# Cross-attention for 16 batches on one core: A of the last heads by 11 block products, and the steps without A in the order of the others

## The chip, the cores and the metric

The kernel runs on one core of a Trainium2 chip. The time is the device time of one execution in microseconds, taken as the median of several runs. The engines are named as the profile names them: PE is TensorE (matmuls; PEld is its weight load), DVE is VectorE, ACT is ScalarE, POOL is GpSimd and SP is SyncE, which issues most DMAs. Each engine works through its own queue in order and waits for the others by semaphores.

## The reference

All is float32, with B = 16 batches, 256 queries of width 256, 77 keys of width 192, and 8 heads of width 256:

```
Q = x @ Wq;  K = c @ Wk;  V = c @ Wv            # split into 8 heads
score = Q K^T / sqrt(256), masked;  attn = softmax(score)
ctx = attn V;  out = ctx @ Wo + x
return layernorm(out) * gamma + beta
```

The kernel never forms Q, K or V. For each head it makes G = Wk Wq^T / 16 once (tiles gA, gB, gC, and sums of their blocks in gS) and U = Wv Wo once (uA, uB). For each batch it makes A = G c (the 256 x 77 matrix whose product with x gives the scores) and VW = c U. A tile is 128 queries of one batch, so a batch is two tiles, and tile t belongs to batch t // 2.

## The kernel before, in words

For one batch the work is this, with the functions' names.

- A for its batch and all heads, made on TensorE for groups of four batches (g = 0 to 3) and pairs of heads. There are two ways. `prepare_fast(g, u)` makes A of a pair of heads for all four batches by a block scheme with 11 products in place of 12 for each head; VectorE puts the blocks together in four additions a head (`put_together`), and ScalarE copies one block a head. `prepare_a` makes it directly, and ScalarE copies the result. The bank is called pf in the first way and pa in the second.
- VW: `prepare_vw(b)`, two parts on TensorE (part_A over 128 rows, part_B over the other 64), then two copies on ScalarE into vw.
- `scores(t)`: TensorE, x against A, into banks ps. `shift(t)`: VectorE subtracts from the bias and takes the minimum. `exponential(t)`: ScalarE, eight activations. `weigh(t)`: VectorE's reciprocal of the sums (rden), then POOL multiplies in two pieces (four for the two tiles of a batch). `turn(t)`: VectorE transposes the result into pT.
- `seven(b)`: the product of the weighted scores of both tiles with VW on TensorE by a scheme of seven block products (banks pm and po). It needs sums of pT blocks (`sums(b)`, four additions on POOL, tile ss) and differences of VW blocks (`differences(b)`, one subtraction on POOL, tile ts). Its first product uses pT and vw alone, its second ss and vw, its third and fourth ss and ts. ScalarE copies pm to m. Then `add_products(b)` on VectorE and `add_blocks(b)` on POOL (five additions) add all to x.
- The last two batches and a last one in halves use `attend` instead, a plain product.
- `finish(t)`: mean and variance, on ScalarE by two activations where `by_act(t)` holds, else on VectorE (bn_stats, bn_aggr). `spread` and `invert` make the reciprocal of the deviation, `normalise(t)` the output row, and SP stores it. `statistics` is finish, spread and invert of a batch.

The schedule is written by hand: instructions are put on each engine's queue in the order in which the text emits them, and the tile framework adds the semaphores. [...]

Up to batch 8 steps come in pairs. `long_step(b)` (odd b) does the scores of batch b + 1, VW of batches b + 1 and b + 2, seven(b), and two calls of prepare_fast for later batches; `short_step(b + 1)` does the scores of batch b + 2 and seven(b + 1). POOL's work in a long step, in the order of the text, is sums(b) (left over from the short step before), weigh of the two tiles of batch b + 1, add_blocks(b - 1), sums(b + 1), add_blocks(b), differences(b + 1), differences(b + 2), and at times the sums of c for the next group (`sums_of_c`); weigh of batch b + 2 follows in the short step. Lists `behind` and `between` hold work that is emitted in the next step.

From batch 9 on (`ready = 9`) a plain loop emits one step for each batch. Steps 9 to 12 make what is missing of A for the last group (heads 4 to 7) with `prepare_a`, in pieces of one pair of heads and two batches, together with VW of two batches in every other step (`ahead`); there differences(b + 1) comes ahead of seven(b) and of the additions. Steps 13 and 14 end with attend.

Of the kernel before, what the change touches and what calls it, by code (L numbers as in the profile page):

```python
# [20 lines left out]
GB = 4  # L21
# [6 lines left out]
def kernel(  # L28
# [14 lines left out]
    B, S, DI = x.shape  # L43
# [3 lines left out]
    NG = B // GB  # L47
    QT = S // P
# [55 lines left out]
    NS = B - GB // 2 - 1  # L104

# [278 lines left out]
    def prepare_vw(b, rest_first=False):  # L384

        vw_of[b] = vwp.tile([P, 4, 2, P], F32, tag="vw", name=f"vw_{b}", bufs=3)
        parts = slice(0, 4) if b < NS else slice(1, 5)
        pv = [ps_mm.tile([P, 2 * DI], F32, tag="mm", name=f"pv_{b}_{k}") for k in range(2)]

        def part_A():  # L390
            for k in range(2):
                for i in range(NM):
                    nc.tensor.matmul(  # L393
                        pv[k][i * BK : (i + 1) * BK],
                        cA[:, b, k * BK : (k + 1) * BK],
                        uA[:, parts, :, i],
                        start=not rest_first,
                        stop=rest_first,
                    )

        def part_B():
            for i in range(NM):
                for k in range(2):
                    nc.tensor.matmul(  # L404
                        pv[k][i * BK : (i + 1) * BK],
                        cB[half(k), b, k * BK : (k + 1) * BK],
                        uB[half(k), parts, :, i],
                        start=rest_first,
                        stop=not rest_first,
                    )  # L410

        def copies():
            return [
                (vw_of[b][:, :, k, :], pv[k].rearrange("p (q d) -> p q d", q=4)) for k in range(2)
            ]

        return part_A, part_B, copies
# [80 lines left out]
    def by_act(t):  # L498
        return t // QT < B - 2 * GB - 1

    def fast(b):
        return b < B - GB - GB // 2
# [146 lines left out]

    def add_seven(b):  # L650

        add_products(b)
        add_blocks(b)
# [485 lines left out]
    def work_of(b, rest_first=False):  # L1139
        g, n = b // GB + 1, b % GB  # L1140
        work = [prepare_vw(b, rest_first)]
        if b <= NS and not fast(b):
            part = (0, 2) if g < NG else (2, GB)
            work.append(prepare_a(NG - 1, (NF // 2 + n % 2,), *part, rest_first))
        return work

# [12 lines left out]

    def turn_x_and_normalise(g, n, old):  # L1160
        turn_some_x(g, n)
        if old:
            normalise(old[1])
# [25 lines left out]
    def long_step(b):  # L1189
# [12 lines left out]
        works = work_of(b + 1) + work_of(b + 2)  # L1202
# [6 lines left out]
        fasts = []  # L1209
        for k in range(2):  # L1210
            fasts.append(prepare_fast(g, n + k))
            if k == 0:
                copy_out(works[:1])
            fasts[k][0]()
            if k == 0:
                copy_out(works[1:])
# [9 lines left out]
        else:  # L1226
# [10 lines left out]
            for k in range(2):  # L1237
                differences(b + 1 + k)
# [8 lines left out]
        fasts[0][1](0)  # L1247
        fasts[0][1](1)
        fasts[1][1](0)
        behind.append(partial(fasts[1][1], 1))  # L1250
# [3 lines left out]
    def short_step(b):  # L1254
# [15 lines left out]
        def last_turn():  # L1270
            turn(new[1])
            sums(b + 1)
# [6 lines left out]
    ready = B - GB - GB // 2 - 1  # L1279
# [5 lines left out]
    for b in range(ready, B - 1):  # L1285
        old = range(max(b - 1, 0) * QT, b * QT)
        now = range(max(b, 0) * QT, (b + 1) * QT)
        new = range((b + 1) * QT, (b + 2) * QT)
# [3 lines left out]
        g, n = (b + 1) // GB + 1, (b + 1) % GB  # L1292
        if g < NG and n % 2 == 0:
            load_x((g * GB + n) // 2)
        alone = b + 1 >= B - GB // 2
        ahead = not alone and n % 2 == 0
        works = work_of(b + 1) if alone or ahead else []
        for part_A, *_ in works:
            part_A()
        for _, part_B, _ in works:  # L1300
            part_B()
# [22 lines left out]
        if ahead:  # L1324
            copy_out(works)
        spread(old[0], old[-1] + 1)
        if ahead:
            works = work_of(b + 2, rest_first=True)
            for _, part_B, _ in works:
                part_B()  # L1330
            for part_A, *_ in works:
                part_A()
        copy_out(works)
        if b + 1 < NS:
            differences(b + 1)
        if ahead and g < NG:
            load_xT(g * GT + n * QT, g * GT + (n + 1) * QT, after_pool=True)
        if b < NS:
            seven(b)
            invert(old[0], old[-1] + 1)  # L1340
            normalise(old[0])
            for t in new:
                turn(t)
            if alone or ahead:
                turn_x_and_normalise(g, n, old)
                if ahead and g < NG:
                    load_xT(g * GT + (n + 1) * QT, g * GT + (n + 2) * QT)
            else:
                behind.append(partial(turn_x_and_normalise, g, n, old))
            if ahead:  # L1350
                sums(b + 1)
            add_seven(b)
            if b + 1 < NS and not ahead:
                sums(b + 1)
            continue
# [53 lines left out]
```

## Time and profile before

| | us |
|---|---|
| median of 3 runs (268.94 to 269.13) | 268.95 |
| the profiled execution | 268.58 |
| its span, first to last instruction | 266.8 |
| TensorE busy in it | 260.5 |
| VectorE busy | 212.7 |
| GpSimd busy | 191.5 |
| ScalarE busy | 166.9 |

The profile is of one execution; its span lies 1.8 us inside its time. A timeline row has its start and its length in us from the start of the span, the engine, the line of the kernel, the operation, the tile written and the tiles read, and a count; consecutive instructions of one kind are one row. A float32 matmul has two records. The chain of waits follows the work that ended last back to the start; its rows in order of time give a start, a length and what ran.

### The profile page before, as it was taken

Reading aid. Unit: us, or ns where it says so; the run is one execution under the profiler, and the core shown is the slowest. Engines: PE = TensorE matmul, PEld = TensorE weight load, DVE = VectorE, ACT = ScalarE, POOL = GpSimd, SP = SyncE. Lnnn points to the kernel's source line nnn. Section 1 sums busy time; section 2 is a strip of 40 time slices with the busy share of each in tenths; the row PEclk is TensorE's granted clock in tenths of the full one; section 3 lists DMA queues with packets and bytes.
Section 4 is the critical chain, followed back from the end, with each engine's and each line's share of the span. In section 5 each row is a group of like instructions: output and inputs, shape, how many; then the busy total and the mean of one; then the engine's idle time right before and its main releaser. Section 6 shows DMA issues by size and latency. Waiting matters only on the chain.

```text
span 266.8 us, 15067 instructions
## 1 busy us (share of the span) xinstructions
PE 260.5 (98%) x6330; PEld 202.8 (76%) x6330; DVE 212.7 (80%) x860; ACT 166.9 (63%) x710; POOL 191.5 (72%) x272
## 2 busy tenths in 40 slices
PE   7999999999999999999999999999999999999992
PEld 6566578948986899679967996799669957985662
DVE  0554968479893789988997969898988798799785
ACT  3253548624584689648983798467964595636772
POOL 1042098799459896899479996997699899685452
PEclk9999999999999999999999999999999999999999
DMA  6999997900240002131314012221234010100112
GB/s 188 209 206 225 335 148 160 300 18 4 63 104 5 2 6 66 58 90 37 83 43 122 5 24 65 81 85 41 54 127 132 20 44 2 44 23 25 42 43 80
DMA packets 41699, 22.73 MB, mean 85 GB/s; under 512 B 24144, under 2 KB 40608, under 8 KB 41632
## 3 DMA queue, kind: packets, MB, share of 16 engines
q1 hardware_dynamic: 41248, 20.98, 31.3%
q0 software_dynamic: 384, 0.79, 1.3%
q8 instruction: 50, 0.82, 1.3%
q14 instruction: 17, 0.14, 0.2%
HBM read 17.57 MB, written 4.19 MB: 82 GB/s over the span
## 4 chain that ended last, share of the span: by engine, by line
PE 96%; DMA 2%; DVE 1%; SPq 0%; issue 0%; DVEq 0%
PE ps L469 25%; PE pf L361 11%; PE po L622 11%; PE pv L393 10%; PE pm L622 9%; PE pv L404 6%; PE pa L203 5%; PE po L555 4%; PE pu L956 3%; PE pa L215 2%; PE pr L429 2%; PE pgb L1017 2%; DMA wq_nat<-in_L_xattn_Wq_dram 2%; PE pw L970 1%; PE pr L440 1%; PE phb L1033 1%
## 5 line engine op out<-in xcount | busy, mean ns | idle before, releaser
L512 ACT ACTIVATE s<-s,top 128x77 f32<-128x77 f32 x256 | 85.2, 346 | 24.5 <-DVE top L486 24.5
L469 PE MATMUL ps<-a,xT 128*32 128x154 f32 x2048 | 70.1, 294 | 0.0
L469 PEld LDWEIGHTS ps<-a,xT 128*32 128x32 f32 x2048 | 65.8, 110 | 2.0 <-issue 1.5
L533 POOL TENSOR_TENSOR p<-s,rden 128x512 f32<-128x512 f32 x64 | 47.7, 769 | 21.9 <-DVE rden L527 21.7
L486 DVE CUSTOM_DVE_ANT_0 s<-ps,bias 128x77 f32<-128x77 f32 x256 | 43.3, 232 | 4.6 <-PE ps L469 4.0
L512 ACT ACTIVATION_READ_ACCUMULATOR s<-s,top 128x1 f32 x224 | 41.9, 187 | 0.0
L373 DVE TENSOR_TENSOR a<-pf,a 128x154 f32<-128x154 f32 x80 | 33.9, 435 | 7.3 <-PE pf L361 4.9
L664 POOL TENSOR_TENSOR xg<-xg,m 128x256 f32<-128x256 f32 x39 | 28.8, 738 | 2.7 <-DVE xg L676 0.7
L543 DVE STREAM_TRANSPOSE pT<-p 128x640 f32<-128x640 f32 x32 | 26.3, 827 | 5.1 <-POOL p L533 5.0
L393 PE MATMUL pv<-uA,cA 128*32 128x512 f32 x256 | 29.6, 593 | 0.0
L1150 ACT COPY vw<-pv 128x512 f32<-128x512 f32 x32 | 17.1, 587 | 14.9 <-PE pv L404 14.9
L760 DVE SCALAR_TENSOR_TENSOR xg<-xg,rstd,bet 128x256 f32<-128x256 f32 x27 | 22.7, 840 | 2.6 <-ACT rstd L711 1.2
L586 POOL TENSOR_TENSOR ts<-vw 128x768 f32<-128x768 f32 x13 | 23.6, 1831 | 0.0
L486 DVE DVE_READ_ACCUMULATOR2_ANT top<- 128x1 f32 x256 | 20.9, 82 | 0.0
L393 PEld LDWEIGHTS pv<-uA,cA 128*32 128x32 f32 x256 | 8.0, 110 | 13.3 <-issue 9.8
L731 DVE SCALAR_TENSOR_TENSOR xg<-xg,mv,gam 128x256 f32<-128x256 f32 x30 | 18.0, 600 | 0.1
L361 PE MATMUL pf<-cT,gS 64*64 64x154 f32 x240 | 17.4, 290 | 0.0
L603 POOL TENSOR_TENSOR ss<-pT 128x256 f32<-128x256 f32 x13 | 9.7, 745 | 9.8 <-DVE pT L543 9.7
L404 PE MATMUL pv<-uB,cB 64*32 64x512 f32 x256 | 16.3, 596 | 0.0
L622 PE MATMUL po<-vr,pT 128*32 128x256 f32 x208 | 16.0, 379 | 0.0
L361 PEld LDWEIGHTS pf<-cT,gS 64*64 64x64 f32 x240 | 15.8, 133 | 0.0
L203 PE MATMUL pa<-cA,gA 128*32 128x308 f32 (+1 forms) x256 | 14.0, 360 | 0.0
(153 smaller groups left out, 543.1 us busy)
## 6 DMA issues: line engine op xcount, KB each, us to landing
xg<-in_x_dram SPq DMA_DIRECT2D x8, 512.0 KB, 4.4
xT<-in_x_dram SPq DMA_DIRECT2D x56, 64.0 KB, 2.7
out_dram<-xg SPq DMA_DIRECT2D x11, 256.0 KB, 2.7
wo<-in_L_xattn_Wo_dram SPq DMA_DIRECT2D x4, 512.0 KB, 7.9
wq_blk<-in_L_xattn_Wq_dram SPq DMA_DIRECT2D x12, 128.0 KB, 4.6
out_dram<-xg SPq DMA_DIRECT2D x10, 128.0 KB, 1.7
wk_blk<-in_L_xattn_Wk_dram SPq DMA_DIRECT2D x12, 96.0 KB, 4.0
wvT<-in_L_xattn_Wv_dram POOLq DMA_DIRECT2D x8, 96.0 KB, 6.3
```

The lines of the kernel that those rows point to most:

```text
L203: nc.tensor.matmul(flat(o[i * BK : (i + 1) * BK]), gA[:, h, cols(dc, i)], flat(cA[:, batches, :]), start=not rest_first and n in opening, ...
L361: nc.tensor.matmul(bank[half(i), n], weight(i), moving, start=start, stop=stop,)
L373: nc.vector.tensor_tensor(out, *of, ALU.add)
L393: nc.tensor.matmul(pv[k][i * BK : (i + 1) * BK], cA[:, b, k * BK : (k + 1) * BK], uA[:, parts, :, i], start=not rest_first, stop=rest_first,)
L404: nc.tensor.matmul(pv[k][i * BK : (i + 1) * BK], cB[half(k), b, k * BK : (k + 1) * BK], uB[half(k), parts, :, i], start=rest_first, stop=n ...
L469: nc.tensor.matmul(ps[m // 2][i * BK : (i + 1) * BK, m % 2 * 2 * S2 : (m % 2 + 1) * 2 * S2], xT_of[t // PT][:, j * NM + m, dc], flat(a_of[ ...
L486: nc.vector.tensor_tensor_reduce(s[:, h], ps[a][:, k * S2 : (k + 1) * S2], bias[:, b, :], scale=-1.0, scalar=FAR, op0=ALU.add, op1=ALU.min ...
L512: nc.scalar.activation(s[:, h], s[:, h], AF.Exp, bias=top[:, one], scale=-1.0, accum_out=den[:, one] if summed_by_act(t) else None,)
L533: nc.gpsimd.tensor_tensor(part, e_mh[:, :, :, keys], rden_mh.unsqueeze(3).to_broadcast(list(part.shape)), ALU.mult,)
L543: nc.vector.transpose(pT_of[t].rearrange("p n m q -> p m n q"), p.rearrange("p m (n k) -> p m n k", k=BK),)
L622: nc.tensor.matmul(out[i * BK : (i + 1) * BK], weight[:, i], moving, start=first and n == 0, stop=final and n == len(terms) - 1,)
L664: nc.gpsimd.tensor_tensor(to, to, what, ALU.add)
```

## The change

The pairs of long and short steps go on to batch 12 (`ready = NS = 13`). Three things follow. The last group's heads 4 to 7 are made by prepare_fast, in long step 9, and the four calls of prepare_a in steps 9 to 12 go. Long step 11, which has no A left to make, emits all else in the order of the other long steps; what belongs to batch 13 in `differences` and `sums` is left out there, since that batch uses attend. And `by_act`, which is tied to `ready`, now holds up to batch 10 in place of batch 6. The branches of the plain loop that served steps 9 to 12 go, with their helpers; steps 13 and 14 stay. The diff, cut to its core:

```diff
+    ready = NS
...
     def by_act(t):
-        return t // QT < B - 2 * GB - 1
-
-    def fast(b):
-        return b < B - GB - GB // 2
+        return t // QT < ready - 2
...
-    def work_of(b, rest_first=False):
-        g, n = b // GB + 1, b % GB
-        work = [prepare_vw(b, rest_first)]
-        if b <= NS and not fast(b):
-            part = (0, 2) if g < NG else (2, GB)
-            work.append(prepare_a(NG - 1, (NF // 2 + n % 2,), *part, rest_first))
-        return work
...
     def long_step(b):
...
-        works = work_of(b + 1) + work_of(b + 2)
+        works = [prepare_vw(b + 1 + k) for k in range(2)]
         for part_A, *_ in works:
             part_A()
         if now:
             seven(b)
         for _, part_B, _ in works:
             part_B()
-        fasts = []
-        for k in range(2):
-            fasts.append(prepare_fast(g, n + k))
-            if k == 0:
-                copy_out(works[:1])
-            fasts[k][0]()
-            if k == 0:
-                copy_out(works[1:])
+        fasts = [prepare_fast(g, n)] if g < NG else []
+        copy_out(works[:1])
+        for products, _ in fasts:
+            products()
+        copy_out(works[1:])
+        if fasts:
+            fasts.append(prepare_fast(g, n + 1))
+            fasts[1][0]()
...
             add_blocks(b - 1)
             turn(new[0])
             add_products(b)
             turn(new[1])
             sums(b + 1)
             add_blocks(b)
             for k in range(2):
-                differences(b + 1 + k)
+                if b + 1 + k < NS:
+                    differences(b + 1 + k)
...
-        fasts[0][1](0)
-        fasts[0][1](1)
-        fasts[1][1](0)
-        behind.append(partial(fasts[1][1], 1))
+        if fasts:
+            fasts[0][1](0)
+            fasts[0][1](1)
+            fasts[1][1](0)
+            behind.append(partial(fasts[1][1], 1))
...
     def short_step(b):
...
             turn(new[1])
-            sums(b + 1)
+            if b + 1 < NS:
+                sums(b + 1)
             add_products(b)
             if b + 1 == ready:
                 add_blocks(b)
...
-    ready = B - GB - GB // 2 - 1
     for b in range(-1, ready, 2):
         long_step(b)
         short_step(b + 1)
...
     for b in range(ready, B - 1):
...
-        alone = b + 1 >= B - GB // 2
-        ahead = not alone and n % 2 == 0
-        works = work_of(b + 1) if alone or ahead else []
+        works = [prepare_vw(b + 1)]
...
-        if b + 1 < NS:
-            differences(b + 1)
-        if ahead and g < NG:
-            load_xT(g * GT + n * QT, g * GT + (n + 1) * QT, after_pool=True)
-        if b < NS:
-            seven(b)
-            invert(old[0], old[-1] + 1)
-            normalise(old[0])
-            for t in new:
-                turn(t)
...
-            if ahead:
-                sums(b + 1)
-            add_seven(b)
-            if b + 1 < NS and not ahead:
-                sums(b + 1)
-            continue
         for t in now:
             attend(t)
```

More of the change, by code (lines that the diff above doesn't have):

```diff
@@ L382, in prepare_fast, with prepare_vw @@
         return products, put_together
-    def prepare_vw(b, rest_first=False):
+    def prepare_vw(b):
         vw_of[b] = vwp.tile([P, 4, 2, P], F32, tag="vw", name=f"vw_{b}", bufs=3)
@@ L396, in part_A @@
                         uA[:, parts, :, i],
-                        start=not rest_first,
-                        stop=rest_first,
+                        start=True,
+                        stop=False,
                     )
@@ L407, in part_B @@
                         uB[half(k), parts, :, i],
-                        start=rest_first,
-                        stop=not rest_first,
+                        start=False,
+                        stop=True,
                     )
@@ L648, in seven @@
         m_of[b] = m
-    def add_seven(b):
-        add_products(b)
-        add_blocks(b)
     def add_products(b):
@@ L1158, in turn_some_x @@
                 transpose_x(to_turn[0] * GT + j)
[L1160 to L1163, printed above, removed]
     assert QT == 2
@@ L1285 @@
     for b in range(ready, B - 1):
-        old = range(max(b - 1, 0) * QT, b * QT)
-        now = range(max(b, 0) * QT, (b + 1) * QT)
-        new = range((b + 1) * QT, (b + 2) * QT)
+        old, now, new = (tiles_of(b + i) for i in (-1, 0, 1))
         scores_and_masks(new, old if b == B - 2 else ())
@@ L1291 @@
             behind.pop(0)()
-        g, n = (b + 1) // GB + 1, (b + 1) % GB
-        if g < NG and n % 2 == 0:
-            load_x((g * GB + n) // 2)
-        alone = b + 1 >= B - GB // 2
-        ahead = not alone and n % 2 == 0
-        works = work_of(b + 1) if alone or ahead else []
-        for part_A, *_ in works:
+        works = [prepare_vw(b + 1)]
+        for part_A, part_B, _ in works:
             part_A()
-        for _, part_B, _ in works:
             part_B()
@@ L1323 @@
             weigh(t)
-        if ahead:
-            copy_out(works)
         spread(old[0], old[-1] + 1)
[L1327 to L1332, printed above, removed]
-        copy_out(works)
-        if b + 1 < NS:
-            differences(b + 1)
-        if ahead and g < NG:
-            load_xT(g * GT + n * QT, g * GT + (n + 1) * QT, after_pool=True)
-        if b < NS:
-            seven(b)
-            invert(old[0], old[-1] + 1)
-            normalise(old[0])
-            for t in new:
-                turn(t)
[L1344 to L1350, printed above, removed]
-                sums(b + 1)
-            add_seven(b)
-            if b + 1 < NS and not ahead:
-                sums(b + 1)
-            continue
+        copy_out(works)
         for t in now:
```

## The prediction

> **What bounds the kernel now.** I read the page first, then the chain of waits in order of time, then the table of windows cut where the chain shows a pair of steps begin.
>
> ```profile
> span 266.8 us, 15067 instructions
> ...
> PE 96%; DMA 2%; DVE 1%; SPq 0%; issue 0%; DVEq 0%
> ...
> 130.01:157.60 27.59, 27.59 (x760) 22.65 (x756) 24.61 (x105) 20.58 (x95) 23.03 (x33) 1.00 0.20 54
> 185.18:210.02 24.84, 24.84 (x713) 20.18 (x708) 21.62 (x101) 16.63 (x84) 20.34 (x29) 1.00 0.35 96
> 210.02:234.86 24.84, 24.84 (x712) 20.18 (x708) 21.48 (x97) 15.81 (x67) 22.03 (x29) 1.00 0.07 25
> 234.86:266.80 31.94, 27.10 (x600) 17.93 (x592) 25.85 (x115) 17.23 (x69) 16.37 (x24) 1.00 0.13 44
> ```
>
> The columns of a window are its length, then the busy time of PE, PEld, DVE, ACT and POOL. TensorE has no gap: it is busy 27.59 of 27.59 us in a long-short pair (the one that begins at 130.01), 24.84 of 24.84 in each of the two pairs of steps that the change rewrites (batches 9 and 10, then 11 and 12), and 27.10 from there to its last product. So the time moves by what TensorE is spared, plus every new wait of TensorE; work on another engine counts only if it makes such a wait.
>
> **What TensorE is spared.** The chain shows the composition of the long-short pair of steps 5 and 6, and of what the first old pair has in its place.
>
> ```profile
> 130.01 4.19 PE ps L469 x128
> 134.19 3.43 PE pv L393 x32
> 137.63 1.75 PE pm L622 x64
> 139.38 2.17 PE po L622 x64
> 141.55 1.88 PE pv L404 x32
> 143.43 5.93 PE pf L361 x176
> 149.35 4.32 PE ps L469 x128
> 153.68 1.75 PE pm L622 x64
> 155.42 2.17 PE po L622 x64
> ...
> 189.37 1.72 PE pv L393 x16
> 191.09 1.05 PE pa L203 x32
> 192.13 1.02 PE pv L404 x16
> 193.15 0.56 PE pa L215 x32
> 193.71 0.86 PE pv L404 x16
> 194.57 0.52 PE pa L215 x32
> 195.09 1.85 PE pv L393 x16
> 196.94 1.05 PE pa L203 x32
> ```
>
> The removed A (pa) costs 1.05 + 0.56 + 0.52 + 1.05 = 3.18 us in a pair, and it is done in both old pairs: 6.36. The added A (pf, 88 matmuls in 176 records) is two calls in one pair: 5.93. The first new pair (9, 10) has all the pieces of the pair at 130.01, so 27.59; the second (11, 12) has the same without pf, 27.59 - 5.93 = 21.66. Together 49.25 against 2 x 24.84 = 49.68: TensorE alone saves 0.43 us. (That is 6.36 - 5.93 = 0.43 from A; the pv and ps pieces differ by a tenth each way and cancel.) The products of seven, scores and the last two batches are the same instructions as before.
>
> **What moves on the other engines.**
>
> ```profile
> L373 DVE TENSOR_TENSOR a<-pf,a 128x154 f32<-128x154 f32 x80 | 33.9, 435 | 7.3 <-PE pf L361 4.9
> ...
> xT<-in_x_dram SPq DMA_DIRECT2D x56, 64.0 KB, 2.7
> ```
>
> The statistics of eight tiles (batches 7 to 10) go from VectorE to ScalarE, since by_act now reaches batch 10; 16 copies of A leave ScalarE and 4 come; 16 additions of put_together come to VectorE, 16 x 0.435 = 7.0 us, all in pair (9, 10). That pair is then the pair at 130.01, with ACT at 20.58 and DVE at 24.61 of 27.59 us, and TensorE had no gap there. Pair (11, 12) drops those 7.0: DVE 24.61 - 7.0 = 17.6 and ACT at most 20.58, of 21.66. I cost both at nothing; what hides them is TensorE's own 27.59 and 21.66. Were ACT not to fit, its excess would be below 1 us. The loads of x (one of 512 KB, eight of 64 KB) are the same nine DMAs. They go past the stores of batch 7 on SP's queue and, through the memset ahead of the first, past the two differences on POOL; so they are issued near the end of pair (9, 10), at about 185.18 + 25 = 210. They land 2.7 us later; the scores that read them are those of batch 14, over 20 us on. Nothing.
>
> **The term that decides: POOL's order in the pair without A.** Count from the start of a pair's first scores, t. In a long step GpSimd runs, in the order of the text: sums(b), weigh twice, add_blocks(b-1), sums(b+1), add_blocks(b), differences(b+1), differences(b+2). The short step's seven(b+1) reads ts of differences(b+1) for its third product. In the old steps differences stood ahead of seven and add_seven; in the new order it comes after them. The timeline of POOL, PE and DVE in the pair at 130.01, and three rows of other pairs:
>
> ```profile
> 81.56 2.71 POOL L533 TENSOR_TENSOR p<-s,rden 128x512 f32<-128x512 f32 x4
> ...
> 137.04 0.70 DVE L459 STREAM_TRANSPOSE vr<-vr 128x512 f32<-128x512 f32 x1
> 137.67 0.15 DVE L527 RECIPROCAL rden<-den 128x8 f32<-128x8 f32 x1
> ...
> 137.90 3.39 POOL L533 TENSOR_TENSOR p<-s,rden 128x512 f32<-128x512 f32 x4 [1.07 <-DVE rden L527]
> 141.25 1.00 POOL L664 TENSOR_TENSOR m<-m 128x128 f32<-128x128 f32 x2
> 142.21 2.34 POOL L664 TENSOR_TENSOR xg<-xg,m 128x256 f32<-128x256 f32 x3
> 144.50 0.73 POOL L603 TENSOR_TENSOR ss<-pT 128x256 f32<-128x256 f32 x1
> ...
> 147.49 0.99 POOL L664 TENSOR_TENSOR m<-m 128x128 f32<-128x128 f32 x2
> 148.44 2.35 POOL L664 TENSOR_TENSOR xg<-xg,m 128x256 f32<-128x256 f32 x3
> 150.75 3.62 POOL L586 TENSOR_TENSOR ts<-vw 128x768 f32<-128x768 f32 x2
> ...
> 154.37 1.06 PE L622 MATMUL pm<-ts,ss 128*32 128x128 f32 x32
> ...
> 170.25 1.07 ACT L1150 COPY vw<-pv 128x512 f32<-128x512 f32 x2 [2.63 <-PE pv L404]
> 178.93 3.62 POOL L586 TENSOR_TENSOR ts<-vw 128x768 f32<-128x768 f32 x2
> ```
>
> From 137.90 on POOL runs without a break to the end of differences. The first of the two (3.62 / 2 = 1.81) ends at 150.75 + 1.81 = 152.56, t + 22.55. TensorE first reads ts at 154.37, t + 24.36. It was in time by 1.81 us, and 5.93 of those 24.36 us were pf. In pair (11, 12) pf is gone and TensorE is there at t + 18.43. On POOL nothing ahead of differences(12) is gone: only what lies behind it (differences(13)) and sums(13) is left out. It starts a little sooner, since the transpose at 137.04 (turn_last), which held the reciprocal and with it weigh by 137.67 - 137.04 = 0.63, has no counterpart in step 11: ts at t + 22.55 - 0.63 = t + 21.92. The wait is 21.92 - 18.43 = 3.49 us. Behind the waiting matmul in TensorE's queue stand the rest of seven(12), the scores of batch 14 and everything to the end; the last window has no gap that could take it up, and its chain ends 4.8 us after the last product in any case.
>
> The bounds: the pair at 157.60 had its first differences done at 178.93 + 1.81 = 180.74, t + 23.14 (POOL had come late into it, by the sums of c); that gives a wait of 4.71. The four multiplications of weigh took 2.71 at 81.56 and 3.39 at 137.90; with 2.71 the wait is 3.49 - 0.68 = 2.81. I take 3.49, by the pair at 130.01, because pair (11, 12), like it, follows a pair that has no sums of c.
>
> What is late next: weigh of batch 13 stands behind differences(12) on POOL, but its product attend(13) comes after the scores of batch 14 and two pv pieces, 4.19 + 1.72 + 1.02 = 6.93 us after the delayed seven(12). It has more room than before.
>
> **The sum.** 268.58 (the profiled execution) - 0.43 + 3.49 = 271.64. The median of the runs is 268.95, 0.37 above the profiled one: 272.0.
>
> **The rivals.**
>
> *The stall also costs TensorE its rate.* The first matmuls of the program run slower than later ones of the same width:
>
> ```profile
> L886 PE MATMUL idle<-const-float32-0.0 128*128 128x128 f32 x14 | 3.3, 430 | 0.8 <-PEq L1395 0.8
> L896 PE MATMUL pt_q<-ident,wq_nat 128*128 128x128 f32 x8 | 1.3, 286 | 0.6 <-DMA wq_nat<-in_L_xattn_Wq_dram 0.6
> ```
>
> After its idle start TensorE needed 3.3 us for 14 records, 0.24 each; the later eight took 1.3, 0.16 each, or about half with the fill of two groups taken off. If an idle stretch of 3.5 us brings that rate back for another 3.3 us, half of it, some 1.7 us, is lost on top: 272.0 + 1.7 = 273.7. For it: the wait is long, and the start shows that a slow state exists. Against: the trace has no other gap above 0.6 us to show that one inside the kernel brings it back, so I can only give it a small chance. [...]
>
> *POOL does differences(12) when its input is there (the other side).* The two copies of vw end at 170.25 + 1.07 = 171.32, t + 13.7 in the pair at 157.60. If differences ran then, ts would be there by t + 16, before t + 18.43, and sums(12), pushed back by 1.81 from 144.50 - 0.63 = t + 13.86 to t + 15.67, would still give the three of its four pieces (0.73 each) that come first in seven by t + 17.9. No wait: 268.95 - 0.43 = 268.5. It decides at one point, whether ts is written before t + 18.43. Against: in both pairs quoted differences stand behind the last add_blocks although vw was there 8 us sooner; an engine here keeps the order of the text.
>
> *POOL shortens by more than I allow.* Without put_together VectorE touches memory less and POOL's pieces might all run at their fastest; the rows at 141.25 to 148.44 are already even (0.73, 1.00, 2.35), so only weigh has room. Wait of 2 us or so: 270.5.
>
> *Another wait adds up*, as the reciprocal of step 11 behind a late ScalarE, which now has the statistics of the two tiles of batch 9 ahead of its exponentials. The pair at 130.01 had the same and weigh did not wait for it, so it would take some 2 us more than any row shows: 274.
>
> **How the numbers follow.** The forecast with its wait of 2.81 to 4.71 (271.3 to 273.2) gets 0.80, the slow rate 0.08, a shorter wait 0.04, another wait 0.03, POOL out of order 0.05. The range 271.2 to 274.2 holds the first two nearly whole and half of another wait, about 0.88, and leaves out the rest. A change below 0.2%, 0.54 us, can't be told from none here. Only POOL out of order ends there: 268.5 is 0.16% below the median, so 0.04 for the same and 0.01 for faster; I add 0.01 to faster for what I have not seen. Slower: 0.94.
>
> **What would show it.** In the changed trace the chain should have pf pieces of 5.9 us at about 199 and none after; ps, pv, seven, pv, ps without a gap from about 212.8 to 230.4; then a gap of TensorE of 3.5 us, 0.9 into seven(12), whose releaser is POOL's differences; and the scores of batch 14 at about 237.9 in place of 234.86. The pair from 185.18 should be 27.59 long. I am wrong if that gap is missing or below 2 us, if a second gap of over 0.5 us stands elsewhere, or if the stretch from the scores of batch 14 to the last product is not 27.1.

## The result and the profile after

The median went from 268.94 to 273.45 us (the runs lie between 272.44 and 274.23), a ratio of 1.0163 with a 95% interval of 1.0148 to 1.0178. The predicted time was 272.0, its range 271.2 to 274.2. The profiled execution took 274.05, its span 272.3; that is 5.47 more than the 268.58 of the profiled execution before.

First the page of the changed kernel: its span and the shares of the chain of waits.

```profile
span 272.3 us, 14916 instructions
...
PE 81%; DVE 10%; POOL 7%; issue 1%; DVEq 0%; POOLq 0%
```

Before, TensorE held 96% of the chain. Now it holds 81%, and VectorE and GpSimd together 17%. Next the windows of the changed kernel, cut about where the pairs begin (columns as in the prediction: length, then busy time of PE, PEld, DVE, ACT and POOL, then the granted clock).

```profile
185.18:212.77 27.59, 27.59 (x764) 22.66 (x756) 23.60 (x104) 20.58 (x95) 21.58 (x29) 1.00 0.24 66
212.77:240.00 27.23, 23.83 (x600) 18.38 (x592) 23.18 (x95) 18.22 (x75) 21.39 (x29) 0.94 0.14 42
240.00:272.30 32.30, 27.02 (x600) 17.53 (x588) 25.36 (x116) 17.73 (x71) 14.97 (x23) 1.00 0.13 43
```

The first new pair is 27.58 long by its scores (185.35 to 212.93) and TensorE fills it. The second, forecast at 21.66 and the wait, is 27.23 long with a mean granted clock of 0.94. From its end TensorE works 27.02 us, as before. The waits of TensorE, and its timeline and GpSimd's around the only long one (the brackets hold the idle time and what ended it):

```profile
PE pm L620 <- POOL ts L584: 3.4, 1, 3.4
```

```profile
233.28 1.80 POOL L584 TENSOR_TENSOR ts<-vw 128x768 f32<-128x768 f32 x1
...
235.13 1.93 PE L620 MATMUL pm<-ts,ss 128*32 128x128 f32 x32 [3.40 <-POOL ts L584]
...
239.75 4.36 PE L470 MATMUL ps<-a,xT 128*32 128x154 f32 x128
```

The wait is where the prediction has it, by the instruction that it names, and 3.40 us long. But the products behind it are slow: 1.93 us for 32 records that take 1.08 elsewhere. The granted clock in steps of 1 us (length, busy time of PE, clock) shows why:

```profile
233.00:234.00 1.00, 0.00 (x0) 1.00 0.03 8
234.00:235.00 1.00, 0.00 (x0) 0.95 0.00 0
235.00:236.00 1.00, 0.86 (x18) 0.50 0.00 0
...
238.00:239.00 1.00, 1.00 (x36) 0.84 0.46 164
```

The clock falls to half at 235.00 - 0.05/0.5 = 234.90 and is full again at 238.00 + 0.16/0.5 = 238.32, after 3.4 us. TensorE is at work for 238.32 - 235.13 = 3.2 of these, so about 1.6 us of its time is lost.

Told along TensorE, the 5.47 us are: 0.35 by which this execution was late at the scores of batch 10, with which the first pair begins (185.35 against 185.00), -0.43 of A, 3.58 of delay by the wait (the idle time and the start of the first product behind it), 1.57 by the half clock, and 0.45 at the end, where 5.29 us instead of 4.84 lie between the last product and the end of the span. That sum closes within 0.05. But it doesn't give the cause: taking the wait away, below, gave back less than 1 us.

**The same stretch along VectorE.** VectorE has three marks there: its first reduction of the exponentials of batch 13 (den), its first subtraction for the scores of batch 14 (shift), and its last normalise, with which the kernel ends. The windows between them, up to the end of the last normalise, of the kernel before:

```profile
232.20:238.25 6.05, 6.05 (x196) 5.68 (x188) 5.84 (x14) 1.18 (x4) 4.08 (x7) 1.00 0.09 28
238.25:263.99 25.74, 23.71 (x498) 14.56 (x488) 22.56 (x110) 17.23 (x69) 13.76 (x20) 1.00 0.13 42
```

and of the changed kernel:

```profile
232.69:241.04 8.35, 5.91 (x136) 4.98 (x140) 7.39 (x13) 3.04 (x11) 6.33 (x8) 0.80 0.10 34
241.04:269.46 28.42, 25.98 (x568) 16.57 (x558) 25.10 (x114) 17.23 (x69) 14.06 (x20) 1.00 0.12 41
```

Before, VectorE is busy 5.84 + 22.56 = 28.40 of 31.79 us, and its busy time (the third in each row) is the one to see: it was almost as full as TensorE. After, it has 7.39 + 25.10 = 32.49, 4.09 more, in 36.77, 4.98 more. Some of this is waiting for TensorE and some is work of its own; the experiments tell how much.

### The profile page after: what moved, and what is told of

The parts are those of the page before. It is cut to its first block, busy times and chain, and to the rows that moved or that the text cites. A ratio compares the mean times of both kernels' runs of the same rounds, so it can differ in the third digit from the quotient of the medians.

```text
span 272.3 us, 14916 instructions
## 1 busy us (share of the span) xinstructions
PE 262.7 (96%) x6250; PEld 204.1 (75%) x6250; DVE 215.6 (79%) x860; ACT 173.5 (64%) x730; POOL 190.6 (70%) x272
## 4 chain that ended last, share of the span: by engine, by line
PE 81%; DVE 10%; POOL 7%; issue 1%; DVEq 0%; POOLq 0%
PE ps L470 20%; PE pf L362 13%; PE po L620 10%; PE pm L620 8%; PE pv L394 8%; PE pv L405 4%; PE pa L204 3%; POOL p L531 3%; PE pu L949 3%; DVE s L487 2%; PE pr L430 2%; PE pgb L1010 2%; DVE pT L541 2%; POOL xg L657 2%; PE pa L216 2%; DVE xg L724 2%
## 5 line engine op out<-in xcount | busy, mean ns | idle before, releaser
L374 DVE TENSOR_TENSOR a<-pf,a 128x154 f32<-128x154 f32 x96 | 40.7, 434 | 9.3 <-PE pf L362 6.4
L362 PE MATMUL pf<-cT,gS 64*64 64x154 f32 x288 | 20.9, 290 | 0.0
L362 PEld LDWEIGHTS pf<-cT,gS 64*64 64x64 f32 x288 | 19.0, 133 | 0.0
L620 PE MATMUL pm<-ts,ss 128*32 128x128 f32 x416 | 14.6, 284 | 3.4 <-POOL ts L584 3.4
L362 PE MATMUL pf<-cB,gB 64*64 64x154 f32 x192 | 16.7, 290 | 0.0
```

The source lines that it names most:

```text
L362: nc.tensor.matmul(bank[half(i), n], weight(i), moving, start=start, stop=stop,)
L374: nc.vector.tensor_tensor(out, *of, ALU.add)
L620: nc.tensor.matmul(out[i * BK : (i + 1) * BK], weight[:, i], moving, start=first and n == 0, stop=final and n == len(terms) - 1,)
```

## The experiments

The kernel before was measured again on the chip of each set: 269.23 us for experiments 1 to 4, 269.11 for 5 to 8 and 269.02 for 9 to 12. Ratios are to that kernel. Beside the changed kernel's own set (268.94) these differ by up to 0.3, so a difference of medians between sets is uncertain by as much. The theory at first was the prediction's: the wait for differences(12), and after the trace the half clock behind it, make the time. The rival on record was that the short pair has no room for this order, so that another wait takes the place of the first.

**1. The differences first.** In the step without A, differences(12) goes ahead of sums(12), so that TensorE finds ts.

```diff
             turn(new[1])
+            if not fasts:
+                differences(b + 1)
             sums(b + 1)
             add_blocks(b)
             for k in range(2):
-                if b + 1 + k < NS:
+                if fasts and b + 1 + k < NS:
                     differences(b + 1 + k)
```

> In the step without A, differences(12) goes ahead of sums(12) on GpSimd; all else as in the changed kernel. Theory 1 (the wait is for GpSimd's order alone): ts is then written by about 228.9 us, TensorE reads it at 231.5, the 3.4 us gap goes, no stretch at half clock, and what is left is the saving of 0.43 us of matmul work: 268.5 us, at most 0.2 more for sums(12) coming 1.8 later. Rival (a pair of 21.7 us is too short for this order, whatever comes first on GpSimd): another wait of 1 to 3 us takes its place at seven(12) or at the transposes before it: 270 to 272 us.

Measured: 272.81 (272.11 to 273.39), ratio 1.013 (1.0109 to 1.0151), only 0.64 below the changed kernel (3.58 above its own kernel before, where the changed one was 4.51 above). Neither expectation held. Its windows, cut as above, and its longest wait of TensorE:

```profile
213.61:235.30 21.69, 21.69 (x584) 16.90 (x580) 17.75 (x86) 17.45 (x74) 17.90 (x25) 1.00 0.13 37
235.30:271.10 35.80, 27.57 (x601) 17.66 (x592) 29.86 (x124) 17.92 (x72) 18.42 (x27) 0.96 0.14 46
```

```profile
PE po L553 <- DVE xg L669: 2.2, 1, 2.2
```

The wait for ts is gone, there is no half clock in the pair (1.00), and the pair is 21.69 long, as forecast (21.66). Yet the rest is 35.80 long where before it was 31.94, with VectorE at 29.86 where it was 25.85, and TensorE now waits 2.2 us for an addition of VectorE to free a bank of po (the kernel's pool of banks, ps_mm, has bufs=8). So the wait alone is not the cause. The windows between VectorE's marks, in this kernel:

```profile
233.17:240.33 7.16, 7.16 (x204) 6.24 (x200) 6.95 (x14) 2.44 (x9) 5.62 (x9) 1.00 0.13 42
240.33:268.29 27.96, 22.54 (x467) 13.29 (x456) 24.97 (x115) 17.61 (x71) 14.77 (x22) 1.00 0.12 41
```

VectorE is busy 6.95 + 24.97 = 31.92 us, 3.52 more than before, and the stretch is 35.12 long, 3.33 more. So the stretch grew by about what was added to VectorE. Its timeline shows what was added:

```profile
233.17 0.80 DVE L523 TENSOR_REDUCE den<-s 128x8 f32<-128x616 f32 x1 [1.03 <-ACT s L510]
...
234.12 0.99 DVE L724 SCALAR_TENSOR_TENSOR xg<-xg,mv,gam 128x256 f32<-128x256 f32 x1
235.15 0.84 DVE L753 SCALAR_TENSOR_TENSOR xg<-xg,rstd,bet 128x256 f32<-128x256 f32 x1
235.91 1.27 DVE L724 SCALAR_TENSOR_TENSOR xg<-xg,mv,gam 128x256 f32<-128x256 f32 x1
237.21 0.48 DVE L753 SCALAR_TENSOR_TENSOR xg<-xg,rstd,bet 128x256 f32<-128x256 f32 x1
...
240.33 0.21 DVE L487 CUSTOM_DVE_ANT_0 s<-ps,bias 128x77 f32<-128x77 f32 x1
```

These four rows are normalise of the two tiles of batch 10, 3.58 us. In the long and short steps it is put off by a list into the next short step; the old loop had done it before this point. Four more such rows, of batch 11, follow at 244.23 to 246.49 (2.2 us). The kernel before has one batch there, batch 11, in two places, 2.5 us in all.

**2. A alone.** Steps 9 and 10 as in the change, steps 11 and 12 in the old order, without A. `by_act` holds up to batch 8.

```diff
     def by_act(t):
-        return t // QT < B - 2 * GB - 1
+        return t // QT < NS - 4
     def fast(b):
-        return b < B - GB - GB // 2
+        return True
...
-    ready = B - GB - GB // 2 - 1
+    ready = NS - 2
```

> The 11-product A alone: steps 9 and 10 as a long and a short step with pf, steps 11 and 12 in the order that they had before, without A. Theory 1: in that order differences(12) ended at 224.8 us and ts was read at 231.6; without 3.2 us of direct A that is still 3.6 us of room, so no wait, 268.94 - 0.43 = 268.5 us. Rival (the eleven products or the pair that carries them cost the time, not the order): slower than 270 us, with a gap in the pair from 185 us or a half clock there.

Measured: 271.64 (271.39 to 271.94), ratio 1.0088 (1.0073 to 1.0103). Apart from its start TensorE has no wait above 0.7 us, and from the scores of batch 10 to those of batch 14 it needs 235.03 - 185.53 = 49.50 us, 0.18 less than before (49.68). VectorE's marks are what moved, by its timeline:

```profile
214.70 0.20 DVE L486 CUSTOM_DVE_ANT_0 s<-ps,bias 128x77 f32<-128x77 f32 x1
...
218.76 0.77 DVE L731 SCALAR_TENSOR_TENSOR xg<-xg,mv,gam 128x256 f32<-128x256 f32 x1
...
231.46 0.22 DVE L486 CUSTOM_DVE_ANT_0 s<-ps,bias 128x77 f32<-128x77 f32 x1
...
235.33 0.76 DVE L525 TENSOR_REDUCE den<-s 128x8 f32<-128x616 f32 x1
```

Its shift of batch 13 starts at 231.46, 45.93 us after the scores of batch 10 (before: 227.87, 42.87), and den 49.80 after them (before 47.20). The 16 additions of the eleven-product A aren't what holds it up: the last of them ends at 212.00, and shift of batch 12 starts at 214.70, 1.59 after TensorE began those scores at 213.11 (before 3.57 after them). It is lost between the two shifts, 16.76 us apart (before 14.46): five tiles' normalise stand there in place of three, the first three of them from 218.76 to 223.28, in a pair that lasts 21.92 us on TensorE in place of 24.84. The plain loop begins with what the pairs have held back (a tile of batch 8 and both of batch 9), and it now begins at step 11, where it did at step 9. This is read from the timeline; no run takes it away. TensorE's 0.43 us buy nothing here.

**3. The gap filled.** 14 products of zeros stand on TensorE where it waited for ts; the wait stays, the idle time goes. They write a bank that nothing reads.

```diff
+        if b == NS - 1:
+            fill = ps_mm.tile([P, P], F32, tag="mm", name="fill")
+            for _ in range(14):
+                nc.tensor.matmul(fill, zeros, zeros, start=True, stop=True)
```

> 14 products of zeros (about 3.0 us at the full rate) stand in seven(12) between the second and the third product, where TensorE waits 3.4 us; they leave the result as it is. Theory 1 with the half clock as a follow-up of the idle gap: ts comes at the same time, the gap shrinks to about 0.5 us, the clock stays at 1.00, and the runs lie within 0.5 us of each other at about 272.3 us. Rival (the spread of the runs and the half clock have another cause, such as the load of the steps before): half clock and a spread of 1.8 us as before, 273 to 274 us.

Measured: 272.84 (272.48 to 273.16), ratio 1.0132 (1.0116 to 1.0149). TensorE's timeline:

```profile
231.39 3.39 PE L636 MATMUL fill<-const-float32-0.0 128*128 128x128 f32 x28
234.85 1.08 PE L620 MATMUL pm<-ts,ss 128*32 128x128 f32 x32
```

The zeros' 28 records take 3.39 us (the expectation's 3.0 was an estimate), and ts is read 0.07 us behind them. The clock stays at 1.00 in each us from 231 to 240, and the runs spread by 0.7 instead of 1.8 us. So in these two traces the half clock comes with the idle time and goes with it, and without the two the median is 0.6 lower, or 0.9 against each set's own kernel before. And the delay of TensorE (the scores of batch 14 at 237.93, 52.85 after those of batch 10, against 49.28 in experiment 1) is worth nothing beside experiment 1: 272.84 against 272.81. VectorE's shift of batch 14 comes 54.85 after the scores of batch 10 here and 54.49 there; it had to finish batch 10 first in both.

**4. Half the wait.** differences(12) after the third of the five additions of add_blocks(11).

```diff
-            add_blocks(b)
+            add_blocks(b, partial(differences, b + 1) if not fasts else None)
...
```

> differences(12) moved ahead by two of the five additions of add_blocks(11) (1.56 us). Theory 1: the wait falls from 3.4 to about 1.9 us. If the half clock needs a gap of some 3.4 us, it goes too: 270.6 us with a small spread. If any gap of this kind brings it, the clock falls for 3.4 us and the time is 271.5 to 272.3 us. Rival (the wait isn't set by ts): the wait stays at 3.4 us, 273.4 us.

Measured: 272.10 (271.93 to 272.62), ratio 1.0103 (1.0086 to 1.012). TensorE's timeline:

```profile
233.84 1.08 PE L620 MATMUL pm<-ts,ss 128*32 128x128 f32 x32 [1.80 <-POOL ts L584]
```

A wait of 1.80 us, no half clock behind it, and a time no longer than that of experiment 1, which has no wait there, but not the 270.6 that was expected: the length of the wait isn't what sets the time.

**5 and 6. Relief for VectorE, and for ScalarE.** Experiment 1 and the output stage of batch 10 on ScalarE and GpSimd, behind the weigh of batch 13:

```diff
-        statistics(tiles_of(b - 1))
+        beside = tiles_of(b - 1) if not fasts else ()
+        statistics(tiles_of(b - 1), beside)
...
-            behind.append(partial(normalise, t))
+            behind.append(partial(normalise, t, aside=t in beside))
...
```

> differences(12) ahead of sums(12) as in e1, and the output stage of batch 10 (centre and scale, two VectorE passes a tile, 3.4 us for both tiles in e1 at 234.1 to 237.7) on ScalarE and GpSimd, behind weigh of both tiles of batch 13. Theory 2 (with the wait gone the end is set by VectorE: two more tiles of output stage and the exponentials of step 12 that start behind ScalarE's statistics; e1 had 29.86 us of VectorE in a tail that took 35.8, before 25.85 in 31.94): the tail loses about 3 us and the time is 269.3 to 269.9 us. Theory 1 (TensorE's wait for ts alone): no change against e1, 272.8 us. Rival (GpSimd takes over as the bound, with 3.7 us more): 271 to 272 us with gaps ahead of VectorE's transposes that POOL releases.

Measured: 271.67 (271.51 to 272.22), ratio 1.0101 (1.0085 to 1.0117). And experiment 1 with the statistics of batches 7 to 10 back on VectorE:

```diff
     def by_act(t):
-        return t // QT < ready - 2
+        return t // QT < B - 2 * GB - 1
```

> e1 with by_act as in the kernel before (statistics of batches 7 to 10 on VectorE). Theory 2, if the ScalarE statistics of batch 10 (2.8 us ahead of the exponentials of step 12) are the larger part: about 2 us faster than e1, 270.8 us. Theory 2, if the later output stage on VectorE is the larger part: within 0.8 us of e1, 272.0 to 272.8, since VectorE gets 0.6 us a tile more. Theory 1: no change.

Measured: 271.68 (271.41 to 272.05), ratio 1.0093 (1.0074 to 1.0112). Each is 2.6 us above its kernel before, where experiment 1 is 3.6 above, so each gives about 1.0 (their intervals just overlap that of experiment 1). Taking 3.58 us of normalise off VectorE thus gives back less than a third of it. In the first, shift follows den after 6.11 us, as before (6.05). In the second den itself comes 1.1 us sooner, since ScalarE no longer has statistics ahead of the exponentials of batch 13: the statistics that were "cost at nothing" did have a price. In experiment 5 GpSimd is next, as the rival in its expectation had it. VectorE's timeline there, then GpSimd's:

```profile
236.65 0.85 DVE L541 STREAM_TRANSPOSE pT<-p 128x640 f32<-128x640 f32 x1 [1.26 <-POOL p L531]
```

```profile
231.50 0.99 POOL L657 TENSOR_TENSOR m<-m 128x128 f32<-128x128 f32 x2
232.45 2.36 POOL L657 TENSOR_TENSOR xg<-xg,m 128x256 f32<-128x256 f32 x3
...
235.25 2.71 POOL L531 TENSOR_TENSOR p<-s,rden 128x512 f32<-128x512 f32 x4
```

weigh of batch 13 (the last row) stands behind add_blocks(11), and VectorE's transpose waits 1.26 us for it.

**7. The order with A made directly.** The new order, but A made directly in long steps 9 and 11, as much in each as an old pair made.

```diff
-        fasts = [prepare_fast(g, n)] if g < NG else []
+        late_a = b + 1 >= NS - 3
+        fasts = [prepare_fast(g, n)] if not late_a else []
+        lo = b + 1 - (NS - 3)
+        direct = [prepare_a(NG - 1, (NF // 2 + k,), lo, lo + 2) for k in range(2)] if late_a else []
...
+        for part_A, part_B, _ in direct:
+            part_A()
+            part_B()
         copy_out(works[:1])
+        copy_out(direct)
```

> The new order for steps 9 to 12, but A of the last two pairs of heads made directly (two calls in long step 9, two in long step 11, 3.2 us each). Each of the two pairs is then 24.8 us of TensorE, as before. Theory 1: TensorE comes to ts 3.2 us later than in the changed kernel, the wait is 0.2 to 0.4 us, no half clock, 269.3 us. Theory 2: the work behind step 11 on VectorE is as in e1, but starts 2.75 us sooner: 272.8 - 2.75 = 270.0 us, VectorE setting the end.

Measured: 272.76 (272.68 to 272.90), ratio 1.0137 (1.0121 to 1.0153). Both theories were wrong here: with none of the last heads' A by eleven products, full clock and a wait for ts of only 0.9 us, the kernel is 3.65 us slower. Not all of this is the order. The same direct A takes TensorE longer in this place: its pieces are 3.73 and 3.84 us in the two pairs (before 3.18 in each), so the pairs have 25.40 and 25.60 us of work in place of 24.84, 1.3 more in all. Two steps of its chain of waits:

```profile
228.36 0.68 ACT a L1135 x3
...
233.91 0.81 DVE den L523
```

The copies of A on ScalarE now stand ahead of the statistics and the exponentials of batch 13, and VectorE's den comes 48.56 us after the scores of batch 10 (before 47.20); 1.09 of these 1.36 us are there already at the scores of batch 13 (42.66 after those of batch 10, before 41.57). The rest of the loss lies behind den and is the order's: 2.39 us by the marks below.

**8. The output stage aside, the wait kept.** The changed kernel with the edit of experiment 5 and without that of experiment 1.

> The output stage of batch 10 on ScalarE and GpSimd as in f1, but differences(12) behind the additions as in the changed kernel. If both limits are there side by side (theory 2), the wait of 3.4 us now decides alone: 272 us with no half clock inside work, up to 273.5 with it, 2.5 to 3.5 us above f1. If the wait is harmless, as fast as f1.

Measured: 273.20 (272.08 to 274.71), ratio 1.0157 (1.0121 to 1.0192). It is 1.5 above experiment 5. Where VectorE has been relieved, the wait does show, though not with its 3.4 us, and not with the 2.5 to 3.5 expected; whether a half clock has a part in the 1.5 isn't shown. Its profiled execution, of 272.08, has the wait without the half clock and is only 0.4 above the median of experiment 5. The half clock isn't all that spreads the runs: that of 273.71 has a mean clock of 1.000. TensorE's timeline, then the clock in steps of 1 us:

```profile
234.72 1.08 PE L620 MATMUL pm<-ts,ss 128*32 128x128 f32 x32 [3.41 <-POOL ts L584]
```

```profile
234.00:235.00 1.00, 0.28 (x12) 1.00 0.00 0
235.00:236.00 1.00, 1.00 (x40) 1.00 0.00 0
```

The same wait, 3.41 us, and no half clock.

**9 to 11. GpSimd's additions later.** add_blocks(11) goes behind the weigh of batch 13, first beside experiment 1, then also with the output stage aside, then also with the statistics on VectorE.

```diff
             sums(b + 1)
-            add_blocks(b)
+            if fasts:
+                add_blocks(b)
...
         weigh(new[1])
+        if b + 1 == ready:
+            add_blocks(b - 1)
...
```

> The kernel with differences(12) first (272.81), and beside it add_blocks(11), about 3.3 us of GpSimd, put behind the two weigh of batch 13 in the short step of batch 12. Theory (three engines in a chain, ScalarE to VectorE to GpSimd, each about full): VectorE still has the output stage of two more tiles in the stretch behind scores(14), so taking 3.3 us from GpSimd alone gives at most what each of the two other single cuts gave, 0 to 1.1 us: 271.7 to 272.8. Rival (GpSimd's order alone is the limit, the work on VectorE only fills its pauses): the 3.3 us come back whole, 269.3 to 270.0.

> The same, and also the output stage of batch 10 on ScalarE and GpSimd behind the weigh of batch 13 (the single cut that gave 271.67, with GpSimd then without a pause from 220.09 to 235.44). Theory (chain): with both VectorE and GpSimd relieved TensorE is the limit again up to the tail: 269.0 to 270.3. Rival (the order costs by something else, such as the weights of batch 13 late because of the statistics on ScalarE): nothing beyond the single cut, 271.3 to 271.8.

> The same, and the statistics of batches 7 to 10 on VectorE as in the kernel before, so that ScalarE has 2.8 us less ahead of the exponentials of batch 13. Theory (chain): 268.4 to 269.4, the kernel before less the 0.43 us of TensorE, with up to 0.9 for the tail; between it and the kernel with the output stage aside the difference is what ScalarE's place in the chain still costs, 0 to 1. Rival (something else in the order): 271 or more.

Measured: 275.33 (275.25 to 277.55), ratio 1.0255 (1.0226 to 1.0283); 274.62 (274.44 to 274.93), ratio 1.0208 (1.0189 to 1.0227); 273.66 (273.11 to 274.02), ratio 1.0164 (1.0145 to 1.0183). No expectation held; the edit made things worse. TensorE's and VectorE's timelines in the first of the three (its profiled execution, of 277.55, lost more further on; the rows lie ahead of that):

```profile
235.50 4.37 PE L470 MATMUL ps<-a,xT 128*32 128x154 f32 x128
```

```profile
242.11 0.43 DVE L684 BATCH_NORM_STATS2 bn<-xg 128x6 f32<-128x256 f32 x1 [3.29 <-POOL xg L657]
...
243.48 0.21 DVE L487 CUSTOM_DVE_ANT_0 s<-ps,bias 128x77 f32<-128x77 f32 x1
```

The statistics of batch 11 read what add_blocks(11) writes, and in VectorE's queue they stand ahead of the shift of batch 14. VectorE now stands for 3.29 us. The scores were there: TensorE began them at 235.50, as early as in experiment 1. So, with TensorE on time at this place, 3.3 us of idle VectorE put its shift of batch 14 2.9 us later (57.38 after the scores of batch 10, against 54.49), and the median is 2.5 higher (275.33 against 272.81). Further on TensorE then waits for VectorE, and its clock falls (its timeline, and the clock in steps of 1 us):

```profile
263.45 3.64 PE L553 MATMUL po<-vw,pT 128*32 128x256 f32 x32 [3.19 <-DVE xg L669]
```

```profile
262.00:263.00 1.00, 0.00 (x0) 0.78 0.00 0
```

How much of the 2.5 is this half clock isn't separated in experiment 9. In experiment 10, whose profiled execution (274.58) is close to its median, shift comes 2.29 us later behind den than in experiment 5 (8.40 against 6.11), and the last part is only 0.30 longer, with slow products in it (32 records into po take 3.13 us from 261.64 on, 32 like them 1.91 at 256.11). So here VectorE's order sets when the last part begins. That is not what the three runs were for: whether all three relieved together, without that new wait, bring the time back was not measured.

**12. The differences twice.** The changed kernel with differences(12) done twice, a longer wait.

```diff
-                    differences(b + 1 + k)
+                    differences(b + 1 + k, 1 if fasts else 2)
...
```

> The changed kernel with differences(12) done twice on GpSimd, so 1.8 us more of it ahead of the products that wait. The output is the same. Wait: 5.2 us in place of 3.4. [...] Rival (the wait is hidden behind the chain of the other engines): under 0.5 us more, unless GpSimd itself is the chain, then 1.8 us more too, without the half clock.

Measured: 277.10 (276.24 to 277.51), ratio 1.0295 (1.0273 to 1.0318), 3.65 above the changed kernel. Its timeline and its clock:

```profile
236.99 1.94 PE L621 MATMUL pm<-ts,ss 128*32 128x128 f32 x32 [5.38 <-POOL ts L585]
...
243.92 0.24 DVE L487 CUSTOM_DVE_ANT_0 s<-ps,bias 128x77 f32<-128x77 f32 x1 [2.29 <-PE ps L470]
```

```profile
234.50:235.50 1.00, 0.00 (x0) 0.97 0.00 0
...
241.50:242.50 1.00, 1.00 (x20) 0.62 0.00 0
```

A wait of 5.38 us, and half clock from 235.44 to 242.26, 6.8 us: twice as long as after the wait of 3.40 in the changed kernel. VectorE waits 2.29 us for TensorE's scores here, so this time the delay counts: 1.98 more of wait and 1.0 more of half clock (5.64 us from the first product behind the wait to the scores of batch 14, against 4.62), where the rival had under 0.5 in all, or 1.8 without a half clock.

**The marks of VectorE together.** For each profiled execution, the starts as rows of the timelines give them, in us: den from the first scores of batch 10 on, shift from den on, the last normalise from shift on, and their sum. They are counted from there because those scores begin anywhere from 184.93 (experiment 8) to 186.18 (experiment 11), a difference that arises ahead of the change. The sum belongs to the profiled execution, whose time stands beside the median.

| kernel | den | shift | last normalise | sum | profiled | median |
|---|---|---|---|---|---|---|
| before | 47.20 | 6.05 | 25.26 | 78.51 | 268.58 | 268.94 |
| after | 47.34 | 8.35 | 27.94 | 83.63 | 274.05 | 273.45 |
| 1, no wait | 47.33 | 7.16 | 27.48 | 81.97 | 272.96 | 272.81 |
| 2, A alone | 49.80 | 6.04 | 24.83 | 80.67 | 271.44 | 271.64 |
| 3, gap filled | 47.33 | 7.52 | 27.49 | 82.34 | 272.48 | 272.84 |
| 4, half the wait | 47.33 | 6.98 | 27.49 | 81.80 | 272.62 | 272.10 |
| 5, output aside | 47.34 | 6.11 | 27.99 | 81.44 | 271.51 | 271.67 |
| 6, statistics back | 46.22 | 7.25 | 27.47 | 80.94 | 272.05 | 271.68 |
| 7, A made directly | 48.56 | 6.23 | 27.47 | 82.26 | 272.79 | 272.76 |
| 8, aside, with the wait | 47.33 | 6.83 | 27.94 | 82.10 | 272.08 | 273.20 |
| 9, additions later | 47.47 | 9.91 | 28.98 | 86.36 | 277.55 | 275.33 |
| 10, and output aside | 47.33 | 8.40 | 28.29 | 84.02 | 274.58 | 274.62 |
| 11, and statistics back | 46.22 | 8.28 | 27.97 | 82.47 | 274.02 | 273.66 |
| 12, differences twice | 47.34 | 11.36 | 27.97 | 86.67 | 276.94 | 277.10 |

The last part is 27.5 us or more in every kernel with the new order and 24.8 to 25.3 in both with the old, with and without a wait of TensorE before it: at least 2.2 us that belong to VectorE's order of work. They can be placed. From the shift of batch 14 to its first reduction for batch 14 VectorE takes 3.99 us before (238.25 to 242.24) and 4.00 in experiment 2, but 6.64 in each of experiments 1, 3 and 7; behind that reduction all four take 20.83 to 20.85, the kernel before 21.27. VectorE's timeline before and in experiment 1:

```profile
236.12 1.56 DVE L543 STREAM_TRANSPOSE pT<-p 128x640 f32<-128x640 f32 x2
237.61 0.71 DVE L676 TENSOR_TENSOR xg<-po,xg 128x256 f32<-128x256 f32 x2
...
242.24 0.76 DVE L525 TENSOR_REDUCE den<-s 128x8 f32<-128x616 f32 x1
```

```profile
241.56 0.84 DVE L541 STREAM_TRANSPOSE pT<-p 128x640 f32<-128x640 f32 x1
242.33 0.71 DVE L669 TENSOR_TENSOR xg<-po,xg 128x256 f32<-128x256 f32 x2
...
246.97 0.76 DVE L523 TENSOR_REDUCE den<-s 128x8 f32<-128x616 f32 x1
```

Before, both transposes of batch 13 and add_products(12) stand ahead of the shift of batch 14, which starts at 238.25; in the new order the second transpose and add_products(12) are held back behind the first tile's shift, and two tiles of batch 11 are normalised there instead of one. That makes up the 2.65 us. The sum of the changed kernel is 5.12 above that of before, 3.46 of which stand in experiment 1 without the wait for ts and without a half clock at work; experiment 3 adds 0.37 for the delay of TensorE, and the other 1.29 are there only with the half clock.

## Why the prediction was right in its number, and where it was wrong

- **What TensorE is spared.** Right: 27.58 for the first pair (27.59 forecast), 21.69 for the second without its wait (21.66), and the pf piece at 198.95 of 5.92 us (5.9 at about 199).
- **The wait.** Right in place, releaser and size: 3.40 us idle and 3.58 of delay against 3.49. The rival in which GpSimd does differences when its input is there is out. In the rival of a shorter wait, that VectorE's use of memory lengthens GpSimd's pieces was an estimate: before, the four multiplications of weigh take 2.71 us at 81.56, where VectorE is busy 1.05 us beside them, and 3.39 at 137.90, where it is busy 3.32, and no run separates the cause.
- **The half clock.** Listed as a rival, 273.7 with a chance of 0.08. It came true in the profiled execution (1.6 us lost against "some 1.7") and the median is 0.6 to 0.9 lower with the gap filled, by experiment 3. The step that failed is the chance: a trace without another gap above 0.6 us tells nothing of a gap of 3.4. That an idle stretch brings the rate of the start back, for 3.3 us, was an estimate from that start alone, whose slow records (14 in 3.3 us) have a granted clock of 1.00 in each of the first 4 us; that the two are one state no run shows. The runs had half clock for 3.42 us with the wait of 3.40 and for 6.82 with that of 5.38, and none with the 3.41 of experiment 8.
- **"I cost both at nothing."** This is the step that failed outright. TensorE's 27.59 and 21.66 hide the amount of work on ScalarE and VectorE, and the budget was about right (17.45 and 17.75 of 21.69 in experiment 1). But it counts only sums within a pair, and the work does not stay in its pair: normalise arrives one batch later, and a transpose and add_products move behind the next shift, in a stretch where VectorE was already busy 28.40 of 31.79 us. Experiment 1 shows the price of the order without the wait, 3.6 us, as much as the wait was forecast to cost; 2.65 of it are the rows behind the shift of batch 14.
- **"The last window has no gap that could take it up, and its chain ends 4.8 us after the last product in any case."** Half wrong. The 27.1 us of TensorE came out (27.02) and the end is 5.29 behind. But the last window has a second limit, VectorE's own 25.85 of 31.94, in the row that the prediction quoted. "Work on another engine counts only if it makes such a wait" is the rule that misled: where the second engine has almost as little room as the first, its order sets the end.
- **What is late next.** "weigh of batch 13 ... has more room than before" holds beside the wait: TensorE doesn't wait for it. Once the wait is gone, experiment 5 has weigh behind add_blocks(11), at 235.25.
- **The sum.** 272.0 against 273.45. That the number is near is in part luck: two causes of about 3.5 us lie beside each other, most of one hides behind the other, and the prediction had one. The missing 1.4 would be the half clock where it falls and the parts of the two that don't overlap; the runs don't separate these. Its signs of error (a gap below 2 us, a second gap above 0.5, a last stretch other than 27.1) all stayed silent, since they look at TensorE alone.

No kernel run here beats the one before; the nearest, A alone, takes 271.64. What the output stage, the statistics and weigh would give when relieved together, without a new wait of VectorE, stays open.

## What to carry to other kernels

Before calling an engine the sole bound, cut the last window at the point where its order changes and add up the second engine's busy time there: if it is nearly full too, what is put off into that window can add to the time, and the first engine need not show a wait for it. A work list that holds things back by one step moves work, not only order; follow each of its pieces to the engine and the window where it lands. When the trace after shows a wait of just the size of the loss, take the wait away before believing it.

## What the runs showed of the hardware

With a wait of 3.40 us the granted clock of TensorE fell to half, for 3.4 us (234.90 to 238.32), in the changed kernel; with a wait of the same length, 3.41 us, in experiment 8 it did not; with 1.80 us in experiment 4 it did not; with 5.38 us in experiment 12 it was at half for 6.8 us (235.44 to 242.26), though TensorE was at work again from 236.99 on. It was at half with a shorter wait too: with the 3.19 us of experiment 9, from 262.56 to 269.38, where TensorE had been at work again since 263.45. Behind the 3.20 us of experiment 10 the products were slow: 32 records took 3.13 us, where 32 like them had taken 1.91 before the wait. The lengths at half clock in the rows are 3.42, 6.82 and 6.82 us, so once or twice about 3.4 us, and they began 0.23, 1.55 and 0.89 us before TensorE's work went on, so their start doesn't follow the kernel. What sets it, and why one wait of 3.4 us had the half clock behind it and another had not, no run shows. Whether the half clock makes the spread from run to run (1.8 us with the gap, 0.7 with the gap filled) isn't shown either: of the changed kernel's runs, those of 272.44 and 274.23 us have the same mean clock, 0.994, and the one of 273.14 has 0.999.
